# One tiled attention run per block instead of two, in a two-layer graph-attention kernel

## The chip, the cores and the metric

The kernel runs on one core of a Trainium2 chip. The metric is the device time of one execution in microseconds (us), and lower is better. TensorE is written PE in the profile, its weight loads PEld, VectorE DVE, ScalarE ACT and GpSimd POOL; SP is the queue from which transfers are issued.

## The reference, cut to what matters

```python
# x: (128, 64, 768) fp32, adj: (128, 64, 64); weights (2, 768, 768); ln_a ones, ln_b zeros
h = relu(layernorm(x))
for l in range(2):
    u_left  = h @ (h @ W_left[l].T).T  / sqrt(768)      # per batch: 64 x 64
    u_right = h @ (h @ W_right[l].T).T / sqrt(768)
    u = upper triangle and diagonal of u_left, lower triangle of u_right
    attention = normalised exp(u) * adj
    ctx = attention @ (h @ W_lin[l].T + b_lin[l])
    h = relu(_layer_norm(ctx, ln_a[l], ln_b[l]))        # divides by (std + 0.001)
return x + h
```

## The kernel before

The 8192 tokens are 16 blocks of 8 batches. A layer has two passes: pass one makes left and right products, scores and attention; pass two makes the linear layer of a block (15 products of a fast matrix multiplication scheme, 8 matmuls of 128 x 256 each) and, in between, the context of the block before. Products accumulate in the PSUM banks X, Y, Z, V. After each product a bank is read into `hl` by ScalarE (first time) or VectorE (later), and a bank that starts with a bias is filled by ScalarE before it is used again. The other engines' work hangs on numbered slots, two to a product; slots from 30 on belong to the next block.

```python
def context(u, r):                        # half r of a block: four quadrants of 64 x 64
    cx = [ps_aux.tile([P, 2, T], F32, name="aux") for _ in range(2)]
    for n in range(2):
        for (j, k, i) in ((lo, 0, lo), (hi, 0, hi), (lo, 1, hi), (hi, 1, lo)):
            m = n if j == lo else 1 - n   # row halves on different banks
            nc.tensor.matmul(cx[k][i, m, :HH], at[j, q, :], hl[j, q, m * HH:(m + 1) * HH], ...)
# ... finish(u, r): squares (ScalarE), deviation, then by slots: inverse, scaled x2, done x2
def done(k):                              # last layer: residual sum and store
    nc.vector.scalar_tensor_tensor(xs[k], zs[k], 0.0, xs[k], op0=ALU.max, op1=ALU.add)
# ... linear(u): for each of 15 products
    #   first half of its matmuls; run(slot 2i); second half; read(bank); run(slot 2i + 1)
# ... the contexts of block u - 1, after products 1 and 8 of block u, and the slots of their work
ends = {0: ((u - 1, 0), (6, 7, 8, 11, 12)), 7: ((u - 1, 1), (20, 21, 22, 30, 30))}
```

An even slot comes ahead of the product's bank read in program order, an odd slot behind it.

## Time and profile before

The time before is 2762.3 us. I cut the profiled execution at the starts of matmuls. (I count blocks and products from 1. Where the prediction or an expectation says "block 0", "blocks 1 to 13", "blocks 3 to 13" or "products 2 to 5", it counts from 0.)

| stage (span 2761.89 us) | length, us |
|---|---|
| start to first product | 15.79 |
| pass one, first layer | 897.48 |
| pass two, first layer | 470.94 |
| pass one, last layer | 895.78 |
| pass two, last layer, to the last matmul | 470.78 |
| tail | 11.11 |

A line of the instruction groups of VectorE, over 2400 to 2660 us: count, busy time, mean ns, and idle time ahead. It is the residual sum.

```profile
L730 DVE SCALAR_TENSOR_TENSOR xr<-z,xr 128x768 f32<-128x768 f32 x36 | 68.3, 1935 | 0.0
```

The next two lines are from the view by stretches: the 15th block of the last layer, and the first half of the last block (which does its products by halves).

```profile
2686.12:2715.31 29.19, 29.19 (x153) 23.59 (x152) 19.90 (x24) 13.43 (x26) 23.65 (x16) 1.00 0.41 111
2715.31:2733.54 18.23, 16.68 (x94) 12.07 (x92) 15.29 (x22) 7.26 (x20) 14.24 (x9) 1.00 0.68 180
```

The 15th block has no gap at all; the half block loses 1.55 us, which is one stop.

### The profile page before, as it was taken

What the parts mean: (1) busy time and instruction counts of PE and PEld (TensorE: products, weight loads), DVE (VectorE), ACT (ScalarE), POOL (GpSimd) and SP (SyncE); (2) the same over time, 40 slices, a digit from 0 to 9 for tenths busy, and PEclk for the clock granted to TensorE, in tenths of its full rate; (3) what the DMA queues carried; (4) which work ended last, traced back from release to release, by engine and by line L of the source; (5) the groups of instructions that cost most, each with busy time, mean ns of one, the idle gap of its engine ahead of it and who ended that gap; (6) DMA issues with size and microseconds to landing.
All of it is one profiled execution on the core that took longest, in us unless ns stands there. A gap on an engine that the chain in (4) does not pass through costs nothing.

```text
span 2761.9 us, 46187 instructions
## 1 busy us (share of the span) xinstructions
PE 2731.4 (99%) x18712; PEld 2337.1 (85%) x18712; DVE 1338.4 (48%) x2250; ACT 842.5 (31%) x1469; POOL 1196.8 (43%) x940
## 2 busy tenths in 40 slices
PE   8999999999999999999999999999999999999998
PEld 6888888888888888888788888888888888888886
DVE  6555445545453332333335444444444335676667
ACT  3222223222321244444521211121121214444443
POOL 4332442223223465565432344223222325887885
PEclk9999999999999999999999999999999999999999
DMA  6423433343232343443555422443234204555655
GB/s 196 127 75 98 122 80 81 93 122 85 75 85 67 95 136 107 123 142 104 151 127 154 101 75 76 107 119 79 75 98 120 59 26 147 163 168 163 178 162 139
DMA packets 234068, 310.80 MB, mean 113 GB/s; under 512 B 54144, under 2 KB 184448, under 8 KB 225664
## 3 DMA queue, kind: packets, MB, share of 16 engines
q1 hardware_dynamic: 233696, 307.45, 40.4%
q8 instruction: 149, 2.44, 0.4%
q14 instruction: 63, 0.52, 0.1%
q10 hardware_dynamic: 160, 0.39, 0.0%
HBM read 202.91 MB, written 104.86 MB: 111 GB/s over the span
## 4 chain that ended last, share of the span: by engine, by line
PE 96%; DVE 2%; ACT 0%; issue 0%; DMA 0%; SPq 0%; DVEq 0%; ACTq 0%
PE X L422 24%; PE V L422 16%; PE Y L422 12%; PE X L752 12%; PE Z L422 8%; PE V L752 8%; PE Y L752 6%; PE aux L449 5%; PE Z L752 4%; PE aux L636 3%; DVE ts L155 0%; DVE wm L463 0%; DVE m L155 0%; DMA x<-in_x_dram 0%; DVE w_l L155 0%
## 5 line engine op out<-in xcount | busy, mean ns | idle before, releaser
L155 POOL TENSOR_TENSOR ts<-ht 128x512 f32<-128x512 f32 x441 | 585.6, 1339 | 1220.2 <-DMA ht<-h 531.5
L200 ACT ACTIVATE m<-X 128x512 f32<-128x512 f32 (+1 forms) x256 | 151.6, 592 | 1100.5 <-PE X L422 583.3
L155 POOL TENSOR_TENSOR ts<-ht,ts 128x512 f32<-128x512 f32 x189 | 249.1, 1325 | 151.0 <-PE X L752 75.9
L155 DVE TENSOR_TENSOR m<-m,V 128x512 f32<-128x512 f32 (+1 forms) x256 | 173.2, 677 | 269.6 <-PE V L422 269.5
L155 DVE TENSOR_TENSOR m<-m,X 128x512 f32<-128x512 f32 (+1 forms) x256 | 162.8, 677 | 249.1 <-PE X L422 248.4
L752 PE MATMUL X<-w_n,ts 128*128 128x256 f32 x1024 | 244.0, 380 | 1.3 <-DVE hl L155 0.7
L422 PE MATMUL X<-ts,w_l 128*128 128x256 f32 x1024 | 242.8, 380 | 1.7 <-POOL w_l L155 1.1
L422 PE MATMUL X<-ts,w_r 128*128 128x252 f32 (+1 forms) x1024 | 238.8, 376 | 0.0
L155 DVE TENSOR_TENSOR m<-m,Z 128x512 f32<-128x512 f32 (+1 forms) x128 | 87.4, 683 | 306.4 <-ACT m L200 247.3
L422 PEld LDWEIGHTS X<-ts,w_l 128*128 128x128 f32 x1024 | 192.0, 190 | 32.2 <-DVE m L155 2.7
L752 PEld LDWEIGHTS X<-w_n,ts 128*128 128x128 f32 x1024 | 191.6, 190 | 32.5 <-issue 2.1
L422 PEld LDWEIGHTS X<-ts,w_r 128*128 128x128 f32 x1024 | 192.0, 190 | 26.0
L268 ACT ACTIVATE ht<-ht,b_col,a_col 128x512 f32<-128x512 f32 x192 | 143.5, 804 | 133.4 <-DMA ht<-h 133.4
L752 PE MATMUL Y<-w_n,ts 128*128 128x256 f32 x768 | 182.5, 379 | 0.0
L422 PE MATMUL Y<-ts,w_l 128*128 128x256 f32 x768 | 181.4, 379 | 0.0
L200 ACT ACTIVATE hl<-X 128x512 f32<-128x512 f32 (+1 forms) x136 | 77.7, 571 | 333.2 <-PE X L752 330.2
L422 PE MATMUL Y<-ts,w_r 128*128 128x252 f32 (+1 forms) x768 | 179.1, 376 | 0.0
L752 PEld LDWEIGHTS Y<-w_n,ts 128*128 128x128 f32 x768 | 145.8, 190 | 20.4 <-issue 0.6
L422 PEld LDWEIGHTS Y<-ts,w_l 128*128 128x128 f32 x768 | 145.9, 190 | 19.8
L422 PEld LDWEIGHTS Y<-ts,w_r 128*128 128x128 f32 x768 | 145.9, 190 | 17.4
L155 DVE TENSOR_TENSOR hl<-hl,X 128x512 f32<-128x512 f32 (+1 forms) x136 | 83.0, 652 | 145.4 <-PE X L752 140.5
L155 DVE TENSOR_TENSOR hl<-hl,V 128x512 f32<-128x512 f32 (+1 forms) x136 | 89.0, 654 | 128.0 <-PE V L752 127.6
(142 smaller groups left out, 4711.4 us busy)
## 6 DMA issues: line engine op xcount, KB each, us to landing
ht<-h SPq DMA_DIRECT2D x63, 1536.0 KB, 7.3
h<-xb SPq DMA_DIRECT2D x124, 384.0 KB, 6.0
z<-z SPq DMA_DIRECT2D x128, 192.0 KB, 2.9
x<-z SPq DMA_DIRECT2D x128, 192.0 KB, 8.3
x<-in_x_dram SPq DMA_DIRECT2D x120, 192.0 KB, 8.5
xr<-in_x_dram SPq DMA_DIRECT2D x120, 192.0 KB, 3.6
out_dram<-xr SPq DMA_DIRECT2D x120, 192.0 KB, 2.6
adj<-in_adj_dram SPq DMA_DIRECT2D x64, 128.0 KB, 2.7
```

The lines of the kernel that those rows point to most:

```text
L155: (eng.tensor_add if sign == "+" else eng.tensor_sub)(o, a, b)
L200: nc.scalar.activation(to(o), p, AF.Copy, scale=1.0 if sign == "+" else -1.0)
L268: nc.scalar.activation(ht, ht, AF.Relu, bias=cols[1][:, c:c + 1], scale=cols[0][:, c:c + 1])
L422: nc.tensor.matmul(p[:, g], w[ORDER[i][0]][:, c, g * P:(g + 1) * P], b()[t][:, c, :].rearrange(bs, s=S)[:, :, :ns], start=(new and g == c ...
L449: nc.tensor.matmul(p[h * S + e:h * S + e + 32, q, e:e + 95], ht[:, c, b * S + e:b * S + e + 32], mb[:, e:e + 95], start=(c == 0), stop=(c ...
L636: nc.tensor.matmul(cx[k][i, m, :HH], at[j, q, :], hl[j, q, m * HH:(m + 1) * HH], start=True, stop=True)
L752: nc.tensor.matmul(p[:, n], b[t][:, c, r * P:(r + 1) * P], w[s][:, c, :], start=(i in FIRST and i not in PRELOAD and n == c == 0), stop=(c ...
```

## The change

Its intent: leaving the 128 x 128 arrangement of the array for the quadrants and coming back costs time at each of the two context runs of a block. In blocks 2 to 14 of each layer one run after the 13th product takes both halves, using banks X and Y and pieces of 512 and 256 columns. In the last layer deviations are taken by halves, and the residual sums of a block move into the first products of the next. At the start, x is loaded alone, one weight sum goes to VectorE, and the sums of right weights move. Some buffers get smaller to make room. The diff, cut to its core:

```diff
-    ORDER = ((8, "X", "ta", "+2"), (5, "Z", "u1", "-0+2"), (0, "X", "u2", "+3"), (1, "Y", "u3", "-3"),
+    ORDER = ((5, "X", "ta", "+2"), (8, "Z", "u1", "-0+2"), (0, "X", "u2", "+3"), (1, "Y", "u3", "-3"),
...
+                nc.sync.dma_start(dram.tile([1, 8], F32, name="first"), XR[0, 0][START[0]][:1, :8])
...
-                for f in ws[:3]:
+                for f in ws[:2]:
                     f()
-                t, w = deque(sums_t((1, 0, 0), nc.vector)), deque([vs[4], vs[3]] + vs[5:])
-                needs = ("tw", "wt", "t", "ttww", "wwww", "w", "tw", "t", "ww", "ww", "", "t", "t", "t", "t")
+                t, w = deque(sums_t((1, 0, 0), nc.vector)), deque(vs[2:])
+                needs = ("t", "wt", "wt", "ttwww", "wwww", "w", "tw", "t", "ww", "ww", "", "t", "t", "t", "t")
...
-                        rs = sums_w(0, "r", nc.gpsimd)
-                        put(16, lambda: hold(M[0][:, 0, 4, 0, :1]))
-                        for n in range(0, len(rs), 3):
-                            put(17 + n // 3, *rs[n:n + 3])
+                        rs, rv = sums_w(0, "r", nc.gpsimd), sums_w(0, "r", nc.vector)
+                        put(24, lambda: hold(TS[1, 0, 0]["tf"][:, 0, :1]))
+                        put(25, *rs[:7])
+                        put_all(31, rv[7:11])
+                        put(35, *rs[11:14])
+                        put(36, *rs[14:])
...
+            def context_block(u):
+                hl, at = HL[u], AT[u]
+                lo, hi = slice(0, S), slice(S, P)
+                aux = [ps_aux.tile([P, 2, T], F32, name="aux") for _ in range(2)]
+                x, y = (ps_st.tile([P, 2 * TH], F32, name=n) for n in "XY")
+                wide = {(1, 0): y, (1, 1): x, (0, 0): aux[0][:, 0], (0, 1): aux[0][:, 1]}
+                parts = {}
+                for r in (1, 0):
+                    for k in range(2):
+                        parts[r, k] = [wide[r, k], aux[1][:, k, r * D:(r + 1) * D]]
+                    rows_at = ((lo, 0, lo), (hi, 0, hi), (lo, 1, hi), (hi, 1, lo))
+                    first = [(j, k, i, int(j == hi)) for j, k, i in rows_at]
+                    then = [(j, k, i, int(j == lo)) for j, k, i in rows_at[1::2] + rows_at[::2]]
+                    for j, k, i, n in first + then:
+                        q = r + 2 * k
+                        nc.tensor.matmul(parts[r, k][n][i], at[j, q, :], hl[j, q, n * T:T + n * D],
+                                         start=True, stop=True)
+                return parts
...
+            def finish_block(u, more):
+                parts = context_block(u)
+                order = ((1, 1), (1, 0), (0, 0), (0, 1))
+                zs = {t: sp.tile([P, H], F32, name="z", bufs=4) for t in order}
+                cut = (slice(0, T), slice(T, H))
+                for t in order[:2]:
+                    nc.vector.tensor_copy(zs[t][:, cut[0]], parts[t][0])
+                    parts[t][0] = zs[t][:, cut[0]]
+                    if t == (1, 1):
+                        AHEAD.append(fresh(l, 0, more))
+                ss = stat.tile([P, Q, 2], F32, name="ssb", bufs=2)
+                sd = stat.tile([P, Q], F32, name="sdb", bufs=2)
+                rs = stat.tile([P, Q], F32, name="rsb", bufs=2)
+                def squares(t):
+                    junk = zs[0, t[1]]
+                    for n in range(2):
+                        nc.scalar.activation(junk[:, cut[n]], parts[t][n], AF.Square,
+                                             accum_out=ss[:, 2 * t[0] + t[1], n:n + 1])
+                def deviation(q):
+                    nc.vector.reduce_sum(sd[:, q], ss[:, q], axis=mybir.AxisListType.X)
+                    nc.scalar.activation(sd[:, q], sd[:, q], AF.Sqrt, bias=floor, scale=1.0 / (H - 1.0))
+                def inverse(q):
+                    nc.vector.tensor_scalar_add(rs[:, q], sd[:, q], EPS_LN)
+                    nc.vector.reciprocal(rs[:, q], rs[:, q])
+                def scaled(t):
+                    by = rs[:, 2 * t[0] + t[1]:2 * t[0] + t[1] + 1]
+                    for n in range(2):
+                        to = zs[t][:, cut[n]]
+                        if last:
+                            nc.vector.scalar_tensor_tensor(to, parts[t][n], by, rows["a"][:, cut[n]],
+                                                           op0=ALU.mult, op1=ALU.mult)
+                        else:
+                            nc.scalar.activation(to, parts[t][n], AF.Copy, scale=by)
+                    if last:
+                        nc.gpsimd.tensor_add(zs[t], zs[t], rows["b"])
+                    else:
+                        kept(u, *t, zs[t])
+                def put_each(slots, f):
+                    for n, t in zip(slots, order):
+                        put(n, lambda t=t: f(t))
+                put_each((25, 26, 28, 29), squares)
+                if not last:
+                    put(30, lambda: deviation(slice(0, Q)))
+                    put(32, lambda: inverse(slice(0, Q)))
+                    put_each((33, 34, 35, 36), scaled)
+                    return
+                for r, slots in ((1, (27, 28)), (0, (30, 32))):
+                    for n, f in zip(slots, (deviation, inverse)):
+                        put(n, lambda f=f, r=r: f(slice(2 * r, 2 * r + 2)))
+                put_each((29, 30, 33, 34), scaled)
+                put_each((34, 36, 38, 40), lambda t: added_to(u, *t, zs[t]))
...
-                    if u:
-                        ends = {0: ((u - 1, 0), (6, 7, 8, 11, 12)), 7: ((u - 1, 1), (20, 21, 22, 30, 30))}
+                    if 0 < u < NB - 2:
+                        ends = {12: (u - 1, None)}
+                    elif u:
+                        ends = ({2: ((u - 1, 0), (10, 11, 12, 15, 16)), 7: ((u - 1, 1), (20, 21, 22, 30, 30))} if last else
+                                {5: ((u - 1, 0), (16, 17, 18)), 11: ((u - 1, 1), (28, 29, 30))})
+                    if last and u:
+                        for r, slot in ((1, 13), (0, 17)) if 12 in ends else ((0, 8), (1, 14)):
+                            put(slot, lambda u=u, r=r: residual(u - 1, r))
...
+                        for r, slot in enumerate((2, 14)):
+                            put(slot, lambda r=r: residual(u - 1, r))
                         ends = ({0: ((u - 1, 0), (12, 13, 15, 19, 21)), 9: ((u - 1, 1), (28, 29, 30, 39, 41))},
-                                {2: ((u, 0), (44, 45, 47, 61, 62))})
+                                {2: ((u, 0), (44, 48, 51, 61, 62))})
```

## The prediction

> **What bounds the kernel now.** I read the page's busy shares first, then its chain of waits.
>
> ```profile
> PE 2731.4 (99%) x18712; PEld 2337.1 (85%) x18712; DVE 1338.4 (48%) x2250; ACT 842.5 (31%) x1469; POOL 1196.8 (43%) x940
> ...
> PE 96%; DVE 2%; ACT 0%; issue 0%; DMA 0%; SPq 0%; DVEq 0%; ACTq 0%
> ```
>
> TensorE carries 96% of the chain that ends last. So only three things can move the time: less array time, fewer gaps in it, or a shorter start and tail. The other engines matter only where they are late with a bank.
>
> Next I took the TensorE timeline of one block of the last layer (start, length, instructions).
>
> ```profile
> 2452.54 1.89 PE L752 MATMUL X<-w_n,ts 128*128 128x256 f32 x8
> 2454.36 1.52 PE L636 MATMUL aux<-hl,at 64*64 64x384 f32 x16
> 2455.81 1.99 PE L752 MATMUL Z<-w_n,ts 128*128 128x256 f32 x8
> 2457.64 1.89 PE L752 MATMUL X<-w_n,ts 128*128 128x256 f32 x8
> ```
>
> A product of 8 instructions starts every 1.727 us elsewhere in the timeline. From the X product's start to the second start after the context run is 2457.64 - 2452.54 = 5.10 us, with two products and one context run in it: the run costs 5.10 - 2 x 1.727 = 1.65 us. The 16 tiled instructions start in four rounds of four quadrants, about 0.322 us apart in the steady rounds, so streaming is 4 x 0.322 = 1.29 us. The remaining 0.36 us is the excursion out of the 128x128 arrangement and back. It is visible as the late start of the run, the 1.46 us before Z, and the 1.83 us (not 1.727) between the starts of Z and X.
>
> The view by stretches gives the block as a whole (stretch, then busy time and count of PE, PEld, DVE, ACT, POOL; clock, DMA share, GB/s).
>
> ```profile
> 2461.20:2490.40 29.20, 29.20 (x154) 23.60 (x153) 19.93 (x24) 13.64 (x26) 23.67 (x15) 1.00 0.55 161
> 1056.20:1085.40 29.20, 29.20 (x154) 23.60 (x153) 8.55 (x16) 12.83 (x24) 17.69 (x15) 1.00 0.35 106
> ```
>
> 29.20 us is 15 x 1.727 + 2 x 1.65 with no gap, in both layers. In the last layer VectorE is 68% and GpSimd 81% busy; in the first 29% and 61%.
>
> Last, the timeline where TensorE does stop: the start and the final block.
>
> ```profile
> 7.89 1.02 DVE L231 BATCH_NORM_STATS2 st<-x 128x6 f32<-128x384 f32 x2 [1.40 <-DMA x<-in_x_dram]
> ...
> 15.79 1.99 PE L422 MATMUL X<-ts,w_l 128*128 128x256 f32 x8 [1.15 <-POOL w_l L155]
> ...
> 24.40 1.96 PE L422 MATMUL X<-ht,w_l 128*128 128x256 f32 x8 [1.41 <-DVE w_l L155]
> ...
> 43.51 1.99 PE L422 MATMUL V<-ts,w_l 128*128 128x256 f32 x8 [1.43 <-DVE m L155]
> ...
> 2732.60 1.10 PE L752 MATMUL V<-w_n,ts 128*128 128x256 f32 x4 [1.55 <-DVE hl L155]
> ...
> 2744.65 1.13 PE L752 MATMUL X<-w_n,ts 128*128 128x256 f32 x4 [0.67 <-DVE hl L155]
> ```
>
> The bracket is the idle time and its releaser. At the start the third piece of x arrives late because weight loads share the queues; then sums of weights hold the first and fifth products, and a slow VectorE the 15th. Near the end VectorE is late twice.
>
> **What the Trainium skill says.** "TensorEngine Tiling (Array Packing)", Key Properties: "Mode switching requires drain", and tiles operate independently. The trace agrees: 0.36 us per excursion, and four quadrants starting within 0.02 us of each other. The same page, Gotcha 1: row tiles cannot access one PSUM bank simultaneously. "PSUM — Partial Sum Buffer", PSUM bank collisions, narrows the measured error to one bank and one 32-partition quadrant. The kernel before keeps row tiles on different banks; the changed one lets them overlap in one bank on different partitions, so this trace cannot test it. "SBUF — State Buffer", Who interferes with whom: a VectorE instruction with two SBUF inputs contends with a GpSimd instruction that reads SBUF. The trace agrees: the residual sum (L730) averages 1.94 us in the block 2461.2 to 2490.4 and 0.95 us alone at 2741.66.
>
> **The change part by part.**
>
> *Context in one run.* In each layer blocks 1 to 13 replace two runs by one after the 13th product: 26 excursions go. The columns are the same per quadrant: two pieces of 512 and two of 256 where there were four of 384. The first order gives one row half 512 and the other 256, the second swaps them. If quadrants advance independently, streaming stays 2 x 1.29 = 2.58 us and the run is 2.58 + 0.36 = 2.94 instead of 3.30: 0.36 saved. I take 0.04 off for quadrants that do not finish together or a weight load that shows. 26 x 0.32 = 8.3 us saved.
>
> *What it adds elsewhere.* Two bank copies of 512 columns on VectorE free X and Y. Priced by the 512-column sums (0.65 us), that is 1.3 us per block; splitting four scalings into eight adds about 0.15 each, 0.6; two small reductions 0.3. VectorE in the last layer goes to about 19.9 + 2.2 = 22 of 28.9 us (76%): still not the bound on average. On ScalarE eight squares replace four, with four more accumulator reads, some 1.2 us in a third-to-half busy engine. The next block's X bank needs its bias. Row half two finishes X about 1.3 us into the run; copy 0.65, bias 0.59 and hops make about 3 us, and X is next needed 2.94 + 2 x 1.73 = 6.4 us into it. Hidden.
>
> Where it is tight: the squares come after the run, then the deviation, and ScalarE's read of product 0's X bank queues behind them. I find that read ending about 9.4 us after the run's start, with product 2 (X again) due at 6.4 + 3.45 = 9.85. In the first layer the scalings stand before the read of product 2's X, again with a few tenths spare. The residual sums at products 2 to 5 can take 1.9 us each beside GpSimd, and the V read they delay is due by product 9. I charge 1.6 us over all blocks for such stops.
>
> *Start.* The small DMA that waits for the first piece of x holds the weight loads back, so x travels alone: at the 370 to 400 GB/s seen in the trace its 1.57 MB should land by about 6.2 us. The VectorE chain then loses its 1.40 us wait, plus the wait of the later normalisations behind it. The first product needs one GpSimd sum instead of three (4.18 us for three). But one weight sum (0.69 us) moves to VectorE, which sets product 5. Gain there: 1.4 - 0.69 + about 1.0 from less contention (VectorE sums took 1.2 to 1.45 us beside GpSimd) = 1.7. The right weights' sums start after the last token sum instead of at 32.4 us, so the slow VectorE behind the 43.5 us stop goes: +1.8 with the small stop at 40. The right weights' sums are now just in time for their products; I take 0.8 back. Net 2.7 us saved.
>
> *Tail and layer border.* Scaling at slots 48 and 51 instead of 45 and 47 lets bank reads pass first: I count the stop of 0.8 us at 2744. The 1.7 us at 2732 has the same residual sums in the same slots, so it stays. Moving the first context of the penultimate step by a product: 0.3 us at the layer border. After the last matmul nothing on the path changes. 1.1 us saved.
>
> Sum: -8.3 + 1.6 - 2.7 - 1.1 = -10.5, from 2762.3 to about 2751.8; I put 2751.5.
>
> **Rivals.**
>
> *The quadrants march in step.* If starts and ends stay in program order, each of four rounds per run lasts as long as its 512-column piece: 4 x 0.86 = 3.44 us instead of 2.58, and a block loses 0.86 - 0.36 = 0.50 us. 26 x 0.5 = +13 us, 2773 with the other parts. Against it: in the trace the second pass of a quadrant starts after the first pass of all four, although a matmul's two passes are emitted together; so quadrants have queues of their own. With equal widths this is suggestive, not proof.
>
> *The freed time turns into bank waits in the last layer.* VectorE and GpSimd are crowded and their contention lengthens both. One stop of 0.5 us per block is 13 x 0.5 = 6.5 us, giving 2757. For it: the 76% and the tight read. Against it: no gap in 29.20 us today, and the context slots leave products 6 to 12 freer than before.
>
> *The start's gain is given back.* The sums of right weights, about 1.3 us each on GpSimd, may hold products 3 to 10 of the second half by 2 to 3 us: 2754. A longer x lead with later weights could do the same.
>
> **Range and chances.** The safe part is 0.36 us per excursion; all working gives 26 x 0.36 + 4 + 1.5 = 15 us, or 2747. Rivals two and three together give 2759. I take 2744 to 2760 for 8 in 10. Two per cent is 55 us; even the marching rival is only 0.4% slower, and the whole of the excursions, start and tail is under 40 us. Within 2%: 0.98.
>
> **What would show it.** In blocks of both layers the period should be about 28.9 us instead of 29.2, with a single tiled run of 32 instructions lasting some 2.94 us start to start. About 3.4 would mean marching; 29.2 or more with gaps before X, Y or V products in the last layer would mean the second rival, with VectorE or ScalarE as releaser. The first product should start near 13.5 us, and the second half of block 0 near 42 us instead of 45.3; x should land by 6.5 us. The stop at 2744 should be gone and that at 2732 still there. Wrong if the time is above 2762, or if the gain comes mainly from outside the 26 blocks.

## The result, and the profile after

The changed kernel takes 2767.54 us (median of four, 2765.0 to 2771.02) against 2762.26 (2761.77 to 2762.69) for the kernel before on the same chip. The ratio is 1.002, with a 95% interval of 1.0003 to 1.0037. A ratio here is formed from both kernels' fast runs of the same rounds, so it is not quite the ratio of the medians. The change is not a gain of 10.8 us but a loss of about 5. The page of its profile:

```profile
PE 2731.5 (99%) x18712; PEld 2349.8 (85%) x18712; DVE 1375.1 (50%) x2372; ACT 857.9 (31%) x1716; POOL 1186.2 (43%) x935
...
PE 8%; DVE 6%; issue 1%; ACT 1%; SPq 0%; DMA 0%; DVEq 0%; ACTq 0%
```

TensorE's busy time is practically the same (2731.5 against 2731.4). The chain line needs care: its shares add up to 16%, because the chain can be followed back only as far as the last layer's pass two. Inside that stretch it alternates between TensorE and VectorE, which had 2% of the whole chain before. The stages say the same (profiled execution, span 2769.24 us; it is the slowest of the four, 3.5 us above the median, so the differences add up to more than the 5 us between the medians):

| stage | before | after | difference |
|---|---|---|---|
| start to first product | 15.79 | 13.37 | -2.42 |
| pass one, first layer | 897.48 | 899.30 | +1.82 |
| pass two, first layer | 470.94 | 466.16 | -4.78 |
| pass one, last layer | 895.78 | 896.11 | +0.33 |
| pass two, last layer, to the last matmul | 470.78 | 483.24 | +12.46 |
| tail | 11.11 | 11.05 | -0.06 |

The view by stretches (columns as in the prediction) shows a block of the first layer, one of the last, the 15th of the last, and the first half of the last block.

```profile
1054.56:1083.40 28.84, 28.84 (x154) 24.05 (x153) 9.83 (x17) 13.46 (x37) 16.65 (x14) 1.00 0.36 115
2449.74:2479.26 29.52, 29.27 (x154) 23.97 (x152) 22.22 (x32) 14.24 (x36) 23.26 (x15) 1.00 0.57 165
2685.88:2721.14 35.26, 31.59 (x153) 24.99 (x152) 27.18 (x37) 15.09 (x35) 26.32 (x16) 0.95 0.41 116
2721.14:2740.03 18.89, 17.01 (x94) 12.28 (x92) 13.05 (x22) 7.26 (x20) 13.04 (x8) 0.98 0.77 202
```

In the first layer the block is 28.84 us without a gap: 0.36 less than 29.20, and 13 such blocks are 4.7 us. In the last layer 0.25 us of a block have no matmul, and at 29.52 us it is longer than before although it has fewer excursions. The 15th block went from 29.19 to 35.26 us, and its mean granted clock is 0.95.

**An ordinary block of the last layer.** The timeline of the changed kernel (start, length) shows how the gap comes about. I picked the lines from the first residual sums to the product that is late.

```profile
2427.41 4.25 DVE L795 SCALAR_TENSOR_TENSOR xr<-z,xr 128x768 f32<-128x768 f32 x2
...
2428.86 1.89 PE L849 MATMUL V<-w_n,ht 128*128 128x256 f32 x8
...
2432.18 2.89 DVE L795 SCALAR_TENSOR_TENSOR xr<-z,xr 128x768 f32<-128x768 f32 x2
...
2434.99 0.67 DVE L155 TENSOR_TENSOR hl<-hl,V 128x512 f32<-128x512 f32 x1
2435.70 0.59 ACT L616 COPY V<-bias 128x512 f32<-128x512 f32 x1 [2.59 <-DVE hl L155]
...
2436.34 1.99 PE L849 MATMUL V<-w_n,ht 128*128 128x256 f32 x8 [0.25 <-ACT V L616]
```

Product 6 writes bank V from 2428.86 on. VectorE would read it about 2 us later, but in its program the second pair of residual sums stands first. The two take 2.89 us together and wait for the pair before them. So V is read at 2434.99. ScalarE puts the bias into V at 2435.70, and product 10 starts 0.25 us late, with one more weight load that couldn't be hidden. The starts of products 9 and 10 are 2.14 us apart instead of 1.73; with a smaller stop at the Y product 3.9 us earlier this makes the 0.67 us between 28.84 and 29.51.

**The context run itself** does what it should. The product ahead of it starts at 2441.63 and the second product after it at 2448.02, so the run is worth 6.39 - 2 x 1.727 = 2.94 us.

**The hand-over near the end.** The 15th block has the two contexts of the 14th in the two-run form while VectorE still has the scalings and sums of the 13th. These are two waits from the timeline.

```profile
2705.10 1.20 DVE L795 SCALAR_TENSOR_TENSOR xr<-z,xr 128x768 f32<-128x768 f32 x1 [2.43 <-DMA xr<-in_x_dram]
...
2710.72 2.51 PE L849 MATMUL X<-w_n,ts 128*128 128x256 f32 x8 [2.07 <-DVE hl L155]
```

VectorE waits 2.43 us for residual rows in the middle of bank reads, then falls behind with the reads, and TensorE stops for 2.07 us. What follows is worse. The profile records the granted clock of TensorE on a grid of 3.413 us. These are two consecutive stretches of that grid; the column behind POOL's counts is the clock.

```profile
2708.64:2712.05 3.41, 1.34 (x7) 1.20 (x7) 3.38 (x6) 0.00 (x0) 3.25 (x4) 1.00 0.69 199
2712.05:2715.46 3.41, 3.41 (x10) 2.71 (x9) 2.19 (x5) 0.38 (x1) 2.34 (x2) 0.50 0.44 150
```

The stop left only 1.34 us of matmuls in the first stretch, and the whole next stretch ran at half clock, which costs half of 3.41, or 1.7 us. The same happens after the stop of 1.88 us at 2738.76, in the last block. The 40 slices of the page do not show it, since they are 69 us wide.

**The start.** The waits that hold products in the first 80 us:

```profile
13.37 1.97 PE L426 MATMUL X<-ts,w_l 128*128 128x256 f32 x8 [0.42 <-DVE ts L155]
...
48.06 1.97 PE L426 MATMUL Y<-ts,w_r 128*128 128x252 f32 x8 [1.31 <-POOL w_r L155]
...
50.38 1.94 PE L426 MATMUL X<-ht,w_r 128*128 128x252 f32 x8 [0.36 <-DVE w_r L155]
...
77.34 1.24 PE L426 MATMUL Z<-ts,w_l 128*128 128x256 f32 x5 [1.39 <-issue]
```

The first product comes 2.42 us earlier, and the stop at 43.5 us has gone. But in the second half of block 1 two products wait for sums of right weights, and at 77.34 a product has a gap inside it for which the view names no releaser. When pass two begins (912.67 against 913.27 us), 0.6 us is left of the gain. Even this may be chance: in ten of the kernels profiled the start is the same to the letter, and their first product starts between 13.37 us (this one) and 14.77, pass two between 912.35 and 914.25 (913.26 on average; the kernel before was profiled once). Ahead of the gap at 77.34 the DMA records show a transfer of 16 KB on an instruction queue (q8, 74.74 to 76.03) and, directly ahead of that, one of 8 KB on another (q14). More on this below.

### The profile page after: what moved, and what is told of

Read it like the earlier page. It is cut to its first block, busy times and chain, and to the rows that moved or that the text cites. A ratio compares the mean times of both kernels' runs of the same rounds, so it can differ in the third digit from the quotient of the medians.

```text
span 2769.2 us, 46496 instructions
## 1 busy us (share of the span) xinstructions
PE 2731.5 (99%) x18712; PEld 2349.8 (85%) x18712; DVE 1375.1 (50%) x2372; ACT 857.9 (31%) x1716; POOL 1186.2 (43%) x935
## 5 line engine op out<-in xcount | busy, mean ns | idle before, releaser
L155 POOL TENSOR_TENSOR ts<-ht 128x512 f32<-128x512 f32 x441 | 573.0, 1311 | 1248.2 <-DMA ht<-h 449.0
L155 POOL TENSOR_TENSOR ts<-ht,ts 128x512 f32<-128x512 f32 x189 | 238.7, 1271 | 135.4 <-PE X L849 60.5
L453 PEld LDWEIGHTS aux<-m,ht 128*32 128x32 f32 x6144 | 126.4, 110 | 15.3 <-issue 15.2
```

The costliest lines, as they stand in the source:

```text
L155: (eng.tensor_add if sign == "+" else eng.tensor_sub)(o, a, b)
L453: nc.tensor.matmul(p[h * S + e:h * S + e + 32, q, e:e + 95], ht[:, c, b * S + e:b * S + e + 32], mb[:, e:e + 95], start=(c == 0), stop=(c ...
```

## The experiments

The theory: all the loss lies in pass two of the last layer. Most of it is VectorE's residual sums, slow beside GpSimd and standing ahead of bank reads, plus a hand-over that collides with the last blocks and the half clock behind its stops. The rivals: the start, the constants or the buffers cost the time; or it is the order alone; or the load alone. All eleven kernels gave correct results. One of the seven runs of the kernel before that stand beside the first four kernels took 2771.27 us (the others 2760.28 to 2761.37). It lowers these four ratios and widens their intervals.

### Undoing parts: the last layer, then both layers

The first kernel puts pass two of the last layer back as it was, and the second does so in both layers, so that only the start and the buffers of the change are left.

```diff
# a1_last_as_before (core of it)
-                    if 0 < u < NB - 2:
+                    if 0 < u < NB - 2 and not last:
# a2_start_only (core of it)
+                    if 0 < u < NB - 2 and False:
# both: residual loads, slots of contexts and the last block as in the kernel before
```

> The changed kernel with the second pass of the last layer put back as it was before (contexts in two runs, residual sums and last block at the old places); the start and the first layer's contexts keep the change. Theory A, the loss lies in the last layer's second pass alone: its 14 middle blocks return to 29.20 us, its length up to the last matmul to about 470.8 us (483.2 in the changed kernel), the first layer keeps its blocks of 28.84 us; total 2755 to 2757.5, some 5 to 7 us under the kernel before. Theory B, the changed start, constants or smaller buffers cost the time and the last layer only shows it (its PE clock fell to half twice): the last layer stays above 476 us and the total above 2762.

Measured: 2756.2 us (2755.78 to 2757.12) against 2760.84, ratio 0.9977 (0.9959 to 0.9996). The first layer keeps 28.84 us, the last layer returns to 29.20 us and 470.12 us in all.

```profile
2709.30:2726.08 16.78, 16.67 (x93) 12.07 (x92) 14.25 (x22) 7.26 (x20) 14.87 (x9) 1.00 0.69 179
```

This is the first half of the last block. It takes 16.78 us where the kernel before took 18.23: the stop at 2732 that I expected to stay has shrunk from 1.71 to 0.27 us (from start to start), although the sums stand where they stood before (the reason is shown with the start, below). The total lies where theory A put it. The loss lies in the last layer, then, and theory B falls.

> Only the start of the change (order of the first products and weight sums, first loads held back, right weights' sums, smaller buffers); contexts of both layers as before. Theory A: the first product starts near 13.4 us, the second half of block 0 near 41.5, and the second pass of the first layer starts 0.6 us earlier than before (912.7 against 913.3), nothing else moves: 2761 to 2762. My prediction's step would have it at 2759.6 (2.7 us saved). Theory B: above 2764.

Measured: 2761.08 us (2760.55 to 2762.09), ratio 0.9994 (0.9972 to 1.0016). The first product starts at 13.95, the second half of block 1 at 42.45, pass two at 913.69 us, each about 0.5 to 1 us later than I expected. The medians (2761.08 against 2760.84) and these positions show no gain. The interval is too wide to exclude the prediction's 2.7 us by the times alone (they would be a ratio of 0.999).

### Order or load: two edits to the residual sums

The third kernel moves each residual sum behind the bank read of its product. The fourth leaves out GpSimd's bias additions in the blocks with one run (`ln_b` is zero, so the result is right, but it isn't a kernel for other inputs).

```diff
# a3_sums_later
-                put_each((34, 36, 38, 40), lambda t: added_to(u, *t, zs[t]))
+                put_each((35, 37, 39, 41), lambda t: added_to(u, *t, zs[t]))
# a4_no_bias_add
-                    if last:
-                        nc.gpsimd.tensor_add(zs[t], zs[t], rows["b"])
-                    else:
+                    if not last:
```

> The changed kernel with one edit: the four residual sums of a block stand one place later in VectorE's order, so behind the bank read of the product instead of ahead of it. Theory order (a bank read queues behind one residual sum of 1.4 to 2.9 us that needn't be ahead of it): blocks 3 to 13 of the last layer fall from 29.51 to about 28.85 us, total about 2760; the stops in the 15th and the last block stay. Theory load (VectorE and GpSimd together are too slow for the stretch, the order doesn't matter): blocks stay at 29.4 to 29.6 and the total at 2766 or more.

> The changed kernel without GpSimd's additions of the layer norm's bias in the blocks with one run (the bias is zero in these inputs, so the result stays right). Theory contention (VectorE's sums are long because GpSimd reads SBUF beside them): the residual sums fall from some 1.9 us towards 0.95 us, the stops before the Y and V products go, blocks 3 to 13 take about 28.85 us, and the total is 2754 to 2760. Theory order alone: the sums get little shorter or the V read stays late, blocks stay above 29.3 us, total 2765 or more.

Measured for the first: 2759.89 us (2757.8 to 2760.72), ratio 0.9989 (0.997 to 1.0008), 7.6 us under the changed kernel (measured in other rounds, in which the kernel before was 1.4 us slower). Blocks 4 to 14 take 28.84 us. The timeline of a block:

```profile
2426.29 1.89 PE L849 MATMUL V<-w_n,ht 128*128 128x256 f32 x8
...
2427.11 2.84 DVE L795 SCALAR_TENSOR_TENSOR xr<-z,xr 128x768 f32<-128x768 f32 x2
...
2429.87 0.67 DVE L155 TENSOR_TENSOR hl<-hl,V 128x512 f32<-128x512 f32 x1
...
2430.47 1.60 DVE L795 SCALAR_TENSOR_TENSOR xr<-z,xr 128x768 f32<-128x768 f32 x1
...
2433.20 1.89 PE L849 MATMUL V<-w_n,ht 128*128 128x256 f32 x8
```

V is now read 3.58 us after product 6 starts, where it was 6.13 us in the changed kernel; the sum at 2430.47 comes behind the read instead of ahead of it, and the V product at 2433.20 has no wait in its bracket.

Measured for the second: 2756.78 us (2755.5 to 2759.14), ratio 0.998 (0.9961 to 0.9999). Blocks 4 to 14 take 28.84 us here too. These are the groups of VectorE's residual sum and of a tiny tensor-scalar instruction of VectorE between 2400 and 2660 us; first the changed kernel, then this one.

```profile
L795 DVE SCALAR_TENSOR_TENSOR xr<-z,xr 128x768 f32<-128x768 f32 x35 | 62.5, 1823 | 0.0
...
L755 DVE TENSOR_SCALAR rsb<-sdb 128x2 f32<-128x2 f32 x18 | 14.1, 781 | 3.3 <-ACT sdb L752 3.3
```

```profile
L793 DVE SCALAR_TENSOR_TENSOR xr<-z,xr 128x768 f32<-128x768 f32 x38 | 34.5, 949 | 0.0
...
L755 DVE TENSOR_SCALAR rsb<-sdb 128x2 f32<-128x2 f32 x18 | 2.9, 163 | 3.3 <-ACT sdb L752 3.3
```

The sum goes from 1823 to 949 ns, and the instruction on 128 x 2 elements from 781 to 163 ns. So nearly half of the sums' time is contention with GpSimd. In the changed kernel 16 of these sums overlap one of the bias additions (2.16 us on average) and 18 overlap GpSimd's sums of tokens (1.48 us); without the additions the sums overlap no GpSimd instruction. The Trainium skill, "SBUF — State Buffer", Who interferes with whom, says that a VectorE instruction with two SBUF inputs contends with a GpSimd instruction that reads SBUF; the residual sums agree. The tiny instruction has one SBUF input, so that sentence does not cover it. Both theories hold in part: neither the slow sum nor its place is enough alone. The kernel before had the same contention (1935 ns) without a stop, and taking away either one removes the stop. In both kernels the 15th block and the last one still lose time (33.21 and 32.10 us for the 15th), and the kernel with later sums has one stretch of half clock, in the last block.

### The hand-over near the end

The next kernel adds to the later sums a spread of the 14th block's contexts and earlier loads of the residual rows. A second one has this edit without the later sums.

```diff
# b1_tail_spread = a3_sums_later plus this; b2_tail_only = the changed kernel plus this
-  {2: ((u - 1, 0), (10, 11, 12, 15, 16)), 7: ((u - 1, 1), (20, 21, 22, 30, 30))} if last else
+  {4: ((u - 1, 0), (13, 14, 15, 19, 21)), 9: ((u - 1, 1), (24, 25, 26, 32, 34))} if last else
# residual loads of the last three half blocks at slots 12 and 22, and 5 of the last block
```

> The run before last (residual sums one place later) with a second edit at the hand-over near the end: the two contexts of the 14th block come at the products 5 and 10 of the 15th block instead of 3 and 8, their residual sums a little later, and the last two loads of residual rows are issued earlier. If the stops in the 15th block (4.4 us there) and in the last block (2.5 us, then 1.7 us at half clock) come from VectorE having three contexts' work in that stretch and from rows that land late, both go: 15th block 29.2 to 30 us, first half of the last block under 17.5 us, no stretch of half clock, total 2750.5 to 2754, under both kernels. If they come from the crowding alone, the stops move: 15th block above 31.5 us, total 2756 or more.

> The changed kernel with the hand-over near the end edited as in the run above, residual sums at their old places. The losses add up: blocks 3 to 13 stay at 29.51 us, the 15th block falls from 35.3 to under 31 us, half clock does not appear, total 2758 to 2760.5, that is about 8 us under the changed kernel, and its runs lie within 2 us of each other instead of 6. If the stops of the 15th block follow from the late reads in the blocks ahead of it, the 15th block stays above 32 us and the total above 2763.

Measured with both edits: 2755.85 us (2755.49 to 2757.13), ratio 0.9977 (0.9963 to 0.999). The 15th block falls to 29.92 us and no half clock is recorded, but the first half of the last block grows to 19.81 us: there my expectation missed, as the stops moved on into the last block in part. Measured without the later sums: 2764.7 us (2763.57 to 2765.37), ratio 1.0009 (0.9995 to 1.0022). The block periods are as expected (29.51 and 29.92 us), and the runs lie within 1.8 us instead of 6. The total is 4 us above the range that I expected, for the same reason: 20.37 us in the half block, with a stop of 2.2 us and one of 1.5.

So I tried to leave the one-run form one block earlier and let the last two blocks run as before.

```diff
# c1_hand_over_early = a3_sums_later plus:
-                    if 0 < u < NB - 2:
+                    if 0 < u < NB - 2 - last:
# block 14 of the last layer: {4: (..., (13, 14, 15, 19, 21)), 9: (..., (24, 25, 26, 32, 34))}
# blocks 15 and 16: contexts and slots as in the kernel before; residual loads at slots of their own
```

> An attempt to beat all: residual sums one place later; the last layer leaves the one-run form one block earlier (12 blocks have it instead of 13), the hand-over block has its two contexts at products 5 and 10, and the 15th and last block run as in the kernel before. Theory (the stops near the end come from three contexts' VectorE work meeting the last block's half-width products): the hand-over block takes about 29.9 us, the 15th block 29.2, the first half of the last under 17 us as in the first run of this study, total 2753.5 to 2755. If VectorE's backlog reaches on into the last block all the same, its first half stays above 18 us and the total at 2755.5 or more.

Measured: 2753.85 us (2752.31 to 2755.87) against 2761.61, ratio 0.9973 (0.996 to 0.9985). The hand-over block, the 15th, and the first half of the last:

```profile
2648.94:2678.87 29.93, 29.46 (x154) 23.58 (x152) 25.83 (x37) 15.39 (x35) 22.86 (x14) 1.00 0.51 144
2678.87:2708.06 29.19, 29.19 (x153) 23.59 (x152) 20.97 (x24) 13.43 (x26) 25.14 (x17) 1.00 0.60 183
2708.06:2725.82 17.76, 16.69 (x94) 12.07 (x93) 14.88 (x22) 7.27 (x20) 15.00 (x9) 1.00 0.72 187
```

The first two are as expected. The half block lies between the two theories (17.76; under 17 or over 18 were named): one stop of 1.24 us (from start to start) is left. Pass two of the last layer takes 467.69 us, 15.6 less than in the changed kernel. This is the fastest kernel; its median is 13.7 us under the changed kernel's (of other rounds) and 7.8 under that of the kernel before.

### The start

Two kernels take parts of the start away: the new place of the right weights' sums, and the small transfer that lets x travel alone.

```diff
# a5_right_as_before = a1_last_as_before with:
-                        rs, rv = sums_w(0, "r", nc.gpsimd), sums_w(0, "r", nc.vector)
-                        ...
+                        rs = sums_w(0, "r", nc.gpsimd)
+                        put(16, lambda: hold(M[0][:, 0, 4, 0, :1]))
+                        for n in range(0, len(rs), 3):
+                            put(17 + n // 3, *rs[n:n + 3])
# c2_no_hold_back = c1_hand_over_early with:
-                nc.sync.dma_start(dram.tile([1, 8], F32, name="first"), XR[0, 0][START[0]][:1, :8])
```

> The changed start and first layer, last layer as before (the first run of this study), with the sums of the right weights back at their old place and all on GpSimd. My prediction: their move saves 1.8 us by taking away the stop at 41.7 us and gives back 0.8. The traces so far: the move takes away 1.6 us and gives back 2.0 at the second half's third and fifth products. Theory given back: the second pass starts within 0.7 us of the first run of this study (912.3), total 2755.5 to 2757. Theory net gain: the stop at 41.7 us returns, the second pass starts 1 us or more later, total above 2757.

Measured: 2756.72 us (2755.44 to 2758.79), ratio 0.9981 (0.9967 to 0.9995). The stop of 1.5 us at the 15th product is back, the two waits in the second half are gone, and pass two begins at 912.13 us against 912.35 for the kernel it is compared with. That fits "given back", but 0.22 us is far below the 1.9 us by which pass two scatters among kernels with one and the same start; what is shown is that the stop and the two waits trade places.

This run also settles why the stop at 2732 went away in the first kernel. Both kernels have the same pass two to the letter, yet here the first half of the last block takes 18.38 us and has the stop (1.70 us), against 16.78. These are the second residual sum of that half block and the GpSimd addition beside it, first in the first kernel, then in this one.

```profile
2723.39 0.94 DVE L795 SCALAR_TENSOR_TENSOR xr<-z,xr 128x768 f32<-128x768 f32 x1
2723.56 2.45 POOL L696 TENSOR_TENSOR ht<-ht,b 128x768 f32<-128x768 f32 x1 [1.57 <-DMA ht<-in_x_dram]
```

```profile
2724.37 1.80 POOL L693 TENSOR_TENSOR ht<-ht,b 128x768 f32<-128x768 f32 x1 [1.31 <-DMA ht<-in_x_dram]
2724.47 2.53 DVE L792 SCALAR_TENSOR_TENSOR xr<-z,xr 128x768 f32<-128x768 f32 x1
```

The addition starts when its rows have landed. Where it started 0.10 us ahead of the sum, the sum took 2.53 us and three bank reads behind it were late; where the sum was 0.17 us ahead, it took 0.94 us and the addition 2.45. In the kernel before the addition is 0.24 us ahead (the sum takes 2.38 us), in the start alone the sum is 0.23 us ahead (0.94). So a few tenths of a microsecond in a landing decide over a stop of 1.7 us, whatever the slots.

> The same kernel without the small transfer that holds the first weight loads back behind the first piece of x. My prediction's working gives that lead about 1.7 us (1.40 us of waiting for x, 1.0 us less contention, less 0.7 us for one sum). If it was worth that at the end, the second pass of the first layer starts 1.5 to 2 us later and the total is 2755 to 2757. If what the lead gains is given back by waits behind it (right weights' sums, and the gap of 1.0 to 1.7 us near 76 us that only kernels with the changed start have), the second pass starts within 0.7 us and the total within 0.8 us of the run beside it, and the gap near 76 us is smaller or absent.

Measured: 2755.42 us (2753.93 to 2758.51), ratio 0.9977 (0.9962 to 0.9992). Pass two begins 0.66 us later than beside it. The medians differ by 1.6 us, but the runs of each kernel spread over more than 3.5 us, and 0.66 us is within the scatter of pass two, so this doesn't decide whether the lead is worth nothing or 1 us. In these two executions there was no lead for the later pieces: the third piece of x landed at 7.26 us without the transfer and at 7.30 with it, the last at 8.26 in both. In the eleven kernels with the transfer the third piece landed between 5.88 us (the changed kernel) and 7.35; in the kernel before it was 7.87.

The part about the gap near 76 us was wrong: it is 1.4 us here and 1.0 beside it. In the other kernels with the changed start it lies between 0.9 and 1.7 us, but in the one with the right weights' sums at their old place it is 0.4, and the kernel before has none. In all twelve kernels that have it, TensorE goes on 1.25 to 1.52 us after the 16 KB transfer on instruction queue q8 has landed. In the eleven with the long gap an 8 KB transfer on q14 comes directly ahead of it; in the one with 0.4 us, and in the kernel before, that transfer comes later (76.71 and 77.95 us). So TensorE may be waiting for its own instructions there, and the move of the sums shifts the other fetch in front of them. This is argued from the times; no run tested it.

### Half clock after a stop, by itself

The kernel of the hand-over gets stops on purpose: extra row sums on VectorE ahead of one bank read in nine blocks.

```diff
# d1_stops: STOPS = {3: 3, 4: 4, 5: 4, 6: 4, 7: 5, 8: 5, 9: 3, 10: 4, 11: 4}
# d2_longer_stops: 6 in the first seven, 7 in the last two
+                        def stop(n):
+                            for _ in range(n):
+                                idle_sum = stat.tile([P, 1], F32, name="idle_sum", bufs=1)
+                                nc.vector.reduce_sum(idle_sum, rows["a"], axis=mybir.AxisListType.X)
+                        put(18, lambda u=u: stop(STOPS[u]))
```

> A measurement, not an improvement: the best kernel so far with stops put in on purpose. In nine blocks of the last layer VectorE does 3 to 5 extra row sums over 768 columns (results unused) ahead of the bank read of the tenth product, so TensorE waits for the bank; the blocks' period differs from the clock record's grid of 3.413 us, so the stops fall at different places in it. Theory half clock: whenever one 3.413 us stretch of that grid holds more than about 1.9 us without matmul, the next stretch is recorded at 0.5 and costs 1.7 us more; stops that are split over two stretches don't do it though just as long. Rival: the length of the stop alone decides, whatever its place; or no stop of this size does it, and the two dips of the changed kernel have another cause. Total about 2754 plus the stops plus 1.7 us for each dip: 2768 to 2790.

Measured: 2764.21 us. The longest stops were 1.77 us, split over two stretches of the clock record, and no half clock was recorded. It told nothing either way, and I had expected a longer time, since VectorE's slack took more of the sums than I thought.

> The same measurement with 6 or 7 sums in each of the nine blocks, as the stops before (0.8 to 1.8 us for 4 and 5 sums) were too short to tell. A sum adds about 1 us, so the stops should be 2.7 us (seven of them) and 3.7 us (two). Theory half clock: a dip follows exactly where more than about 1.9 us of one 3.413 us stretch of the grid are idle, some three to six of the nine; a stop of 2.7 us that the grid splits evenly has none. Rival, length alone: all nine or none. Total 2754 + 26 + 1.7 us per dip, 2785 to 2792.

Measured: 2795.79 us (expected 2785 to 2792). Seven of nine stops were followed by half clock, one more than I had named as the most. Two stops of the same 2.75 us, in stretches of the clock record's grid (the fields as before: TensorE's busy time comes second, the clock third from the end):

```profile
2449.30:2452.71 3.41, 1.34 (x6) 1.24 (x7) 3.38 (x6) 0.00 (x0) 3.41 (x4) 1.00 1.00 281
2452.71:2456.12 3.41, 3.41 (x19) 1.57 (x22) 1.00 (x2) 0.00 (x0) 1.90 (x2) 0.50 0.72 304
2480.02:2483.43 3.41, 2.06 (x10) 1.48 (x8) 3.27 (x5) 0.00 (x0) 3.41 (x4) 1.00 0.95 258
2483.43:2486.84 3.41, 2.00 (x12) 1.54 (x16) 3.06 (x5) 0.00 (x0) 3.38 (x3) 1.00 0.98 287
2486.84:2490.25 3.41, 3.41 (x36) 2.00 (x37) 1.98 (x3) 1.23 (x4) 1.27 (x1) 1.00 0.61 256
```

The stop of the first two lines left 1.34 us of matmuls in one stretch, so 2.07 us were idle, and the next stretch ran at 0.50. The stop of the last three lines lay across a border and left 2.06 and 2.00 us of matmuls, and the clock stayed at 1.00. Of the seven stops of this length, the five with 2.07 us or more idle in one stretch were followed by half clock, and the two with at most 1.41 and 1.85 were not. Their blocks take 33.46 and 31.83 us, so a dip costs 1.63. The length of the stop alone falls as a cause. The limit lies near 1.9 us: in the changed kernel 1.88 us were followed by a dip, in the kernel with later sums 2.31 were, in the kernel without bias additions 1.89 were not, and the ends of matmuls are modelled, so it can't be told finer.

This agrees with the Trainium skill, "TensorE: Matmul & The Clock Gate", Part 1: The HAM clock gate, where the window runs freely, is 3413 ns long and the clock is either full or half. It doesn't agree with that page's rule of thumb (HAM oscillation — how this bites in real kernels) that only gaps of more than about 3.4 us matter: here a bit over half of a window idle was enough, and 1.9 us in the wrong place did it.

## Why the prediction was wrong

**The gain of the runs: right.** The prediction took 0.36 us per excursion and a run of 2.94 us. Both layers show it: 28.84 us per block in the first layer, and in the last as soon as nothing stops it. The 0.04 us that I took off for unequal quadrants wasn't needed. The first rival, quadrants marching in step, is ruled out by the run of 2.94 us.

**The first step that failed:** "The residual sums at products 2 to 5 can take 1.9 us each beside GpSimd, and the V read they delay is due by product 9. I charge 1.6 us over all blocks for such stops." The mechanism was named down to the bank and the product, and it was the second rival as well. But the term was mis-sized: the stops take 0.67 us in each of blocks 4 to 14, 7.4 us in all, where 1.6 was charged. I had only looked at the average load (76%) and at the free products, and did not add up the queue ahead of that one read: four sums of 1.75, 2.58, 0.95 and 2.02 us among the reads of the 3rd to 6th products (the "1.4 to 2.9 us" for one sum takes a line of two sums for one). Moving the sums by one slot, and nothing else, brought these blocks back to 28.84 us.

**The second step that failed** is one that has no term in the sum: the hand-over from one run per block to two in the 15th block. I had priced only the last block's slots. The 15th block lost 6.07 us and the last block 1.6; of these 7.6 us, two stretches of half clock are some 3.4. The spread hand-over alone brought pass two of the last layer from 483.24 to 477.5 us; later sums and the earlier hand-over together brought it to 467.69, without half clock. Whether the dips also explain that the changed kernel's four runs spread over 6 us is not shown: only profiled executions have a clock record by stretch, and kernels without a dip in their profiles spread over 1.3 to 4.6 us, the kernel before once over 11.0.

**The third step that failed:** "Net 2.7 us saved" at the start. The positions came out as said: first product 13.37 us (predicted 13.5), second half of block 1 at 41.49 (predicted 42). In part this was luck: x had landed at 7.32 us and not by 6.5, and with the same start other kernels had their first product up to 1.4 us later. The right weights' sums gave back 2.0 us instead of 0.8, and a gap of 1.5 us near 76 us was added that nothing in the profile before announced. Alone, the start measured a ratio of 0.9994 (0.9972 to 1.0016), which holds both 1 and the 2.7 us.

**The tail.** The stop at 2744 was counted as 0.8 us to be saved and shrank to 0.2, which is right. "The 1.7 us at 2732 has the same residual sums in the same slots, so it stays" was wrong as an argument: it grew to 2.05 us (from start to start; 1.71 before) and drew a half clock behind it, and in the kernel with the last layer's old order it fell to 0.27 us, with the sums in the same slots. In the changed kernel's trace VectorE waits 2.63 us there for residual rows to land (at 2734.94). In the other kernels it hangs on which of VectorE and GpSimd is first, as shown with the start: in the kernel that hands over earlier the second sum took 1.91 us, beside an addition, and 1.24 us of the stop are left. The slots alone do not set it.

**The sum.** In the profiled executions the start was to give -2.7 us up to pass two, and gave -0.6. The first layer's 13 blocks were to give -4.2 of the -8.3, and its pass two gave -4.78. For the last layer I had -4.2 + 1.6 - 0.8 = -3.4, against +12.46: 3.4 from blocks 4 to 14 (7.4 of stops less 4.0 saved), 6.07 and 1.6 from the last two blocks, and 1.3 from the first three, which no experiment looked into. The last layer alone turns the sign. "Within 2%" was right, and the range of 2744 to 2760 missed the 2767.5 us on the high side, above the 2762 that the prediction itself had named as the sign of being wrong.

## What to carry to other kernels

When a change makes the bound engine's work shorter, look at every in-order queue whose items move: add up what stands ahead of each bank read that has a deadline, at the durations under contention, rather than the average load. Give the transition blocks (first, last, where the schedule changes form) a term of their own. A stop of about 2 us of TensorE can cost 1.7 us more than its length, so removing one can be worth more than its gap shows. And take the scatter of positions from several profiles of one start before reading half a microsecond from a single one: here it was 1.4 us at the first product and 1.9 us at pass two.

## What the Trainium skill lacked or had wrong

- "TensorE: Matmul & The Clock Gate": its rule that idle gaps over about 3.4 us matter is too generous. In the run with longer stops, a stop of 2.75 us brought half clock for one stretch of 3.413 us when 2.07 us or more of one stretch were idle, and did not when at most 1.85 were; each such dip cost 1.63 us. The page also tells of half clock from many small gaps, but has no figure for the idle share that is enough; the runs put it near 1.9 of 3.413 us.
- "TensorEngine Tiling (Array Packing)": it says that a change of tiling mode drains the array but gives no cost. Here an excursion to quadrants of 64 x 64 and back cost 0.36 us (29.20 against 28.84 us per block, in all first-layer blocks with one run).
- The same page, Gotcha 1, says that different row tiles cannot use one PSUM bank at the same time. The changed kernel lets row halves write one bank on different partitions: in the run at 2443.45 two matmuls of 512 columns start on bank Y at 2443.93 and 2443.94. The ten kernels that contain this run gave correct results. The narrower statement of "PSUM — Partial Sum Buffer" (one bank and one quadrant of partitions) is the one that fits.
- "SBUF — State Buffer", Who interferes with whom: the direction is right, but it has no size for this mix. A two-input sum of 128 x 768 took 1823 ns on average beside GpSimd's work and 949 ns when it overlapped none, and of such a sum and a GpSimd addition that started 0.10 to 0.24 us apart the later one took 1.3 to 2.7 times as long; a tensor-scalar instruction on 128 x 2 elements, with one SBUF input, took 781 and 163 ns.
